# Layer one's steps in another order: turned maxima, weighted values, scores, energies

## The chip, the cores and the metric

The kernel runs on one core of one Trainium2 chip. The metric is the device time of one execution in microseconds. Three executions took 1420.77, 1421.62 and 1421.86 us; the median is 1421.62 us.

The engines have short names throughout: PE is TensorE (PEld its weight loads), DVE is VectorE, ACT is ScalarE, POOL is GpSimd, SP is SyncE, which here only issues DMAs.

## The reference

Two layers work on x with 32 batches of 128 tokens and 512 features, with a condition of 512 features per batch. Only the first layer's attention is touched by the change.

```python
def L0(hidden, w, ...):                       # layer one, 16 heads of 32 features
    h = sln(hidden, w)                        # LayerNorm, scaled and shifted by the condition
    qkv = (h @ Wqkv.T + bqkv).reshape(B, N, 16, 32, 3)
    energy = einsum('bhqd,bhkd->bhqk', q, k)
    att = softmax(energy, axis=-1) / D ** 0.5
    out = einsum('bhqk,bhkd->bhqd', att, v).reshape(B, N, D) @ Wp.T + bp
    h1 = out + hidden
    return sln(h1, w) + h1

def L1(x, cond, ...):                         # layer two, one head of 512 features, then an MLP
    x = x + attention(film(rmsnorm(x), cond)) @ proj_w + proj_b
    return x + gelu(film(rmsnorm(x), cond) @ mlp_w1 + mlp_b1) @ mlp_w2 + mlp_b2
```

## The kernel before

Batches are worked in eight groups of four (`G = 4`, `NG = 8`). Dense products are made from numbers split in two parts (a high part in a short format and the rest): `mm3` (line 152) issues three matmuls for each of four blocks of the contraction, twelve matmuls of 128x512 for one result. Layer one's attention runs over 32 steps; step `s` treats four heads of one group of four batches (`g, c = divmod(s, KC)`).

The stages of one attention step are functions, and in the same loop body stand the stages of other steps and of other batches, so that TensorE always has something to do:

- `qk0(s)` makes queries and keys of the step's four heads (24 matmuls, two ACT activations into `qk`); it runs two steps ahead. `values0(b)` makes the values of a batch, three batches ahead.
- `energies(s)` multiplies queries and keys with the query on the partitions, 16 small matmuls into four PSUM banks (`pse`), one for each head; the loop takes the four heads in turn for each batch. DVE reduces each bank to negative maxima (`nm`). It runs one step ahead.
- `totals(s, r)` lets ACT take the exponentials of one bank only for their sums: four activations with an accumulated sum each.
- `logs(s)` turns sums and maxima into one number for each row (two ACT instructions, five small ones on DVE, into `nmx`); `maxima(s)` turns that table with a TensorE transpose into the PSUM tile `psm`, and `spread_maxima(s)` copies it four times on DVE into `mT`.
- `scores0(s)` computes the same energies once more with the key on the partitions: first a matmul that subtracts the numbers of `mT`, then 16 small matmuls on top, in four banks `pst`. `exponentials(s, rs)` takes their exponentials on ACT; they are the weights, already divided.
- `heads_out(s)` multiplies weights and values (16 matmuls into one bank `pso`); `heads_high(s)` is ACT's copy of its high part, `heads_low(s)` DVE's rest of it. They are done one step later, in step `s + 1`.
- `End` is the projection of one finished batch: `stream` is a product of twelve matmuls into `psp`, `add` adds the input to it on DVE, and `first`, `sums`, `second`, `third` are the second normalization, in the step after (`past`).
- `Turned` prepares a coming batch: `stats`, `norm` on DVE with a power on POOL; `halves`, an ACT copy and a transposing DMA; a step later `merge` on DVE and four ACT activations in `rest`; a step after that `high` and `low` on DVE (`turned`).
- `Weights` prepares the second layer's weights in steps 4 to 27: `heads` copies on ACT, `tails` and `sums` work on POOL, and each head and tail is stored by a DMA on SP.

The order of instructions on PE, DVE, ACT and POOL is the order of the program (`tc.manual_schedule`); SP's DMAs are placed by a planner. The engines run in order, each waits for what its next instruction needs. A tile's buffer is taken from its pool when the program asks for it, and the first instruction that writes it waits until the last reader of the earlier tile in that buffer is done; which of the free buffers it is, the planner picks. PSUM's eight banks are three pools:

```python
ps_mm = ...tile_pool(name="ps_mm", bufs=2, ...)   # mm_tile
ps_s  = ...tile_pool(name="ps_s", bufs=2, ...)    # s_tile
ps_e  = ...tile_pool(name="ps_e", bufs=4, ...)    # e_bank
```

Before, a step asks for `pst` 0 and 1, `pso`, `psq` from `ps_mm`; for `pst` 2 and 3, `psk`, `psv` from `ps_s`; for four `pse`, `psm`, `psp` from `ps_e`.

Of the kernel before, what the change touches and what calls it, by code (L numbers as in the profile page):

```python
# [16 lines left out]
B, N, D = 32, 128, 512  # L17
P = 128
KC = D // P
# [3 lines left out]
G = 4  # L23
# [20 lines left out]
def cond_seq_kernel(ctx: ExitStack, tc, x, condT, wcond, w0, w1, wk1, wm1, wm2, cols, rows, out):  # L44
# [15 lines left out]
    def mm_tile(name):  # L60
        return ps_mm.tile([P, D], FP, tag="mm", name=name)
# [90 lines left out]
    def mm3(make, terms, done=None, by_part=False):  # L152

        if by_part:
            order = PARTS if by_part == "left" else RIGHT_LOW_LAST
            calls = [(a[pa], b[pb]) for pa, pb in order for a, b in terms]
        else:
            calls = [(a[pa], b[pb]) for a, b in terms for pa, pb in PARTS]
        n = len(calls)
        st = {}  # L160

        def call(j):
            if j == 0:
                st["ps"] = make()
            nc.tensor.matmul(st["ps"], *calls[j], start=(j == 0), stop=(j == n - 1))  # L165
            if j == n - 1 and done:
                done(st["ps"])

        return [lambda j=j: call(j) for j in range(n)]
# [9 lines left out]
    def run(*streams):  # L179

        order = sorted(
            ((j + 0.5) / len(s), i, j) for i, s in enumerate(streams) for j in range(len(s))
        )
        for _, i, j in order:
            streams[i][j]()
# [349 lines left out]
    def values0(b, by_part=False, make=None):  # L535
        g, i = divmod(b, G)
        hT = hs[0, g][0]

        def done(ps):
            if i == 0:  # L540
                vs[g] = w_tile(f"v{g}", FP)
            nc.scalar.copy(vs[g][:, i], ps)

        return mm3(
            lambda: (make or s_tile)(f"psv{b}"),
            [(sub(hT, k, ts(i, P)), sub(W0["v"], k)) for k in range(KC)],
            done, by_part,
        )

    def qk0(s, by_part=False):  # L550

        g, c = divmod(s, KC)
        hT = hs[0, g][0]
        qk[s] = d_tile(f"qk{s}", FP)
        streams = []
        for a, (nm, bias) in enumerate((("q", C_BQ0), ("k", C_BK0))):
            def done(ps, a=a, bias=bias):
                nc.scalar.activation(
                    qk[s][:, a], ps, AF.Identity, bias=col[:, bias + c : bias + c + 1], scale=1.0
                )  # L560

            streams.append(mm3(
                lambda nm=nm: (s_tile if nm == "k" and s > 1 else mm_tile)(f"ps{nm}{s}"),
                [(sub(W0[nm], k, ts(c, P)), sub(hT, k)) for k in range(KC)],
                done, by_part,
            ))
        return streams
# [89 lines left out]
    def heads_out(s):  # L657

        g, c = divmod(s, KC)
        e, v = es.pop(s), vs[g]  # L660
        if c == 0:
            os_[g] = w_pair(f"o{g}")
        pso = mm_tile(f"pso{s}")
        for i in range(G):
            for r in range(4):
                rr = slice(32 * r, 32 * r + 32)
                nc.tensor.matmul(  # L667
                    pso[rr, ts(i, P)], v[:, i, 32 * (4 * c + r) : 32 * (4 * c + r) + 32],
                    e[r][:, ts(i, P)], start=True, stop=True,
                )  # L670
        es[s] = pso
# [12 lines left out]
    class End:  # L684
# [15 lines left out]
        def stream(self):  # L700
            g, i = divmod(self.b, G)

            def done(ps):
                self.ps = ps

            return mm3(
                lambda: e_bank(f"psp{self.b}"),
                [(sub(os_[g], k, ts(i, P)), sub(W0["p"], k)) for k in range(KC)],
                done, "left" if i == 0 else False,
            )  # L710

        def add(self):
# [68 lines left out]
    def l1_vp(a, bb, c, make):  # L781

        if c == 0:
            W1["vp"] = w_pair("w1vp")
        ps = make(f"psvp{c}")
        for k in range(KC):
            nc.tensor.matmul(ps, a[:, k], bb[k], start=(k == 0), stop=(k == KC - 1))
        split_ps(W1["vp"], (slice(None), c), ps)
# [427 lines left out]
    STEPS = KC * NG  # L1216
# [14 lines left out]
    with tc.manual_schedule(engines=ordered):  # L1231
# [85 lines left out]
        new.norm()  # L1317
        run(k)
        new.halves()
        values = values0(2, make=mm_tile)  # L1320
        run(values[:4])
        maxima(0)
        spread_maxima(0)
        first[1].turn()
        run(values[4:])
        first[1].parts()
        W0["p"] = w_pair("w0p")

# [38 lines left out]
        def vp_load(c):  # L1367
            chunk[c] = l1_chunk(2, c)

        def vp(c):  # L1370
            l1_vp(chunk.pop(c), L1[3], c, s_tile if c < 3 else e_bank)

        FIRST1 = STEPS - G - 2

# [10 lines left out]
        for s in range(STEPS):  # L1385
            last = s == STEPS - 1
            end = End(s - G, True, nc.scalar) if s >= G else None
            scores0(s)
            if turned:
                turned.high(nc.vector.tensor_copy)  # L1390
                turned.low(nc.vector)
                turned = None
            if not last:
                energies(s + 1)
            exponentials(s, (0, 1))
            wn, wj = divmod(s - W_FIRST, W_STEPS)
            if 0 <= wn < KC:
                weights.heads(wj)
                weights.tails(wj)
                weights.sums(wj + 1)  # L1400
            if not last:
                totals(s + 1, 0)
            exponentials(s, (2, 3))
            if not last:
                for r in range(1, 4):
                    totals(s + 1, r)
            if s:
                heads_out(s - 1)
            if s == STEPS - 2:
                vp_load(2)  # L1410
            if past:
                past.first()
                past.sums()
            if new:
                new.stats()
            if end:
                end.bias()
                end.more()
            wn, wj = divmod(s + 1 - W_FIRST, W_STEPS)
            if 0 <= wn < KC and wj == 0:  # L1420
                weights = Weights(wn)
            if past:
                past.second()
            if ready and not last:
                ready.merge()
            if s == STEPS - 3:
                vp_load(1)
            if not last:
                logs(s + 1)
            if s:  # L1430
                heads_high(s - 1)
            q, k = qk0(s + 2, (s + 2) % KC == 0) if s + 2 < STEPS else ([], [])
            run(q)
            if staged:
                staged()
            if s < KC:
                split_w(W0["p"], raw["p"], s, nc.gpsimd)
            if s == KC + 1:
                cond_features()
            run(k)  # L1440
            if new:
                new.norm()
                new.halves()
            values = values0(s - 1 + G, make=e_bank if s < G else s_tile) if s <= B - G else []
            run(values[:9] if s < G else values)
            if s == STEPS - 3:
                vp(0)
            if s == STEPS - 2:
                vp(1)
                vp_load(3)  # L1450
                vp(2)
            if s == STEPS - 1:
                vp(3)
            if not last:
                maxima(s + 1)
                spread_maxima(s + 1)
            if s < G:
                run(values[9:])
            if s:
                heads_low(s - 1)  # L1460
            if ready and not last:
                ready.rest()
            if past:
                past.third()
            if "cq" in L1:
                L1.pop("cq")()
            staged = extras[s + 1]() if s + 1 in extras else None
            if end:
                run(end.stream())
                end.add()  # L1470
            if s == STEPS - 4:
                vp_load(0)
            coming_new = None if last else coming(s + 1)
            q2, late = divmod(s - W_FIRST, 3)
            if not late and 0 <= q2 < 4:
                nc.scalar.dma_start(out=w2d[q2], in_=wm2[:, q2])
            if not last:
                turned, ready, new = ready, new, coming_new
            past = end
            if s in CQ:  # L1480
                L1["cq"] = l1_cq(CQ.index(s))
            if s == 2:
                later["mods"] = r_tile("mods")
            if s == STEPS - 2:
                l1_load()
        heads_out(STEPS - 1)
        heads_high(STEPS - 1)
        heads_low(STEPS - 1)
        past.first()
        past.sums()  # L1490
# [191 lines left out]
```

## Time and profile before

| | |
|---|---|
| median of three executions | 1421.62 us |
| the profiled execution, time | 1421.69 us |
| its span in the profile | 1419.9 us |
| mean granted TensorE clock | 0.999 |
| busy: PE, PEld | 1402.5 us (99%), 1135.1 us (80%) |
| busy: DVE, ACT, POOL | 997.2 us (70%), 886.8 us (62%), 384.9 us (27%) |
| chain that ended last | PE 87%, DMA 4%, ACT 4%, DVE 3% |
| first score matmul of steps 0, 1, 2, 3 | 50.1, 63.2, 77.2, 92.6 us |
| of steps 4, 5, 6, 28, 31 | 107.6, 126.0, 142.8, 463.6, 510.8 us |
| `heads_out` of the last step, behind the loop | 520.4 us |

A row of the timeline or of a group names the line of the kernel, the engine, the operation, what is written and what is read (`pso<-e,v`), and the shapes. The number behind x says how many instructions a row stands for. In brackets stands the time that the engine sat idle before it, and what ended that; "issue" means that the profile shows nothing that was waited for. A row of the waits names who waited, for whom, then the total in us, the number of times and the longest. PE's matmuls overlap, and their ends are modelled, so the starts of its weight loads tell more than its busy share.

### The profile page before, as it was taken

The numbers are of one execution on the slowest core, as the hardware profiler recorded it, in microseconds if no ns is written. First come the engines' busy times: TensorE is split into PE (matmuls) and PEld (weight loads), VectorE is DVE, ScalarE is ACT, GpSimd is POOL, SyncE is SP. The second block draws the span as 40 slices with busy tenths as digits, with TensorE's granted clock in tenths as the row PEclk, the third lists the DMA queues.
The fourth block names the chain that finished last, engine by engine and source line by source line (L and its number), as shares of the span: only waits on it lengthen the run. The fifth ranks groups of instructions, "written<-read, shape, count | busy, mean of one in ns | idle before, by whom it ended". The sixth has DMA issues, their size and how long they took to land.

```text
span 1419.9 us, 25300 instructions
## 1 busy us (share of the span) xinstructions
PE 1402.5 (99%) x8968; PEld 1135.1 (80%) x8968; DVE 997.2 (70%) x1970; ACT 886.8 (62%) x2386; POOL 384.9 (27%) x361
## 2 busy tenths in 40 slices
PE   9999999999999999999999999999999999999998
PEld 5766888888888768888888888888888888888887
DVE  6666888888888887999887766665576556753342
ACT  4898899999998856677874454444453445423331
POOL 0113443535444234665541213000030003110000
PEclk9999999999999999999999999999999999999999
DMA  8359778777666557788879878576693767735350
GB/s 310 74 143 238 196 217 225 223 200 187 183 154 183 150 203 187 193 240 222 207 191 361 256 222 260 192 227 195 213 326 121 234 203 227 270 133 184 142 185 30
DMA packets 227879, 287.85 MB, mean 203 GB/s; under 512 B 107396, under 2 KB 138244, under 8 KB 226216
## 3 DMA queue, kind: packets, MB, share of 16 engines
q1 hardware_dynamic: 209888, 211.68, 51.5%
q10 hardware_dynamic: 17864, 74.55, 15.8%
q8 instruction: 70, 1.15, 0.4%
q14 instruction: 57, 0.47, 0.1%
HBM read 193.18 MB, written 73.60 MB: 188 GB/s over the span
## 4 chain that ended last, share of the span: by engine, by line
PE 87%; DMA 4%; ACT 4%; DVE 3%; issue 1%; POOL 1%; SPq 0%; ACTq 0%; POOLq 0%; DVEq 0%
PE acc L1087 24%; PE psh L165 21%; PE psp L165 6%; PE psq L165 5%; PE psk L165 5%; PE psV L165 5%; PE psv L165 5%; PE psT L165 5%; PE pso L667 2%; PE pss L848 2%; PE pse L575 2%; PE pst L644 2%; PE pso L165 1%; ACT unused L599 1%; DMA wc<-in_wcond 1%
## 5 line engine op out<-in xcount | busy, mean ns | idle before, releaser
L599 ACT ACTIVATE unused<-pse,nm 128x128 f32<-128x128 f32 x512 | 180.9, 417 | 10.3 <-DVE nm L588 7.9
L338 POOL TENSOR_TENSOR rn<-vn,neghalf 128x1 f32<-128x1 f32 x96 | 62.9, 655 | 453.3 <-DVE vn L336 346.4
L1025 ACT ACTIVATE c<-c,col 128x512 f32<-128x512 f32 x64 | 46.4, 725 | 142.3 <-DVE c L1050 89.0
L599 ACT ACTIVATION_READ_ACCUMULATOR unused<-pse,nm 128x1 f32 x512 | 131.8, 257 | 0.0
L423 ACT COPY tn<-x 128x1024 uint16<-128x1024 uint16 x90 | 94.1, 1047 | 59.2 <-DVE x L409 51.9
L432 DVE COPY tn<-tn 128x1024 uint16<-128x1024 uint16 x90 | 101.6, 1129 | 6.2 <-DMA tn<-tn 6.1
L1103 POOL TENSOR_TENSOR xe<-xe,row 128x512 f32<-128x512 f32 x32 | 45.4, 1449 | 202.8 <-DMA xe<-xs 182.9
L654 ACT ACTIVATE e<-pst 128x512 f32<-128x512 f32 x128 | 69.7, 605 | 30.1 <-PE pst L644 30.1
L588 DVE TENSOR_REDUCE nm<-pse 128x4 f32<-128x512 f32 x128 | 79.5, 684 | 11.8 <-PE pse L575 11.8
L963 POOL TENSOR_TENSOR wml<-wm,wmh 128x512 fp32r<-128x512 f32 x28 | 35.9, 1287 | 182.4 <-ACT wmh L956 154.9
L1040 DVE TENSOR_TENSOR c<-psh,ca 128x512 f32<-128x512 f32 x32 | 22.1, 692 | 86.7 <-PE psh L165 83.2
L326 DVE BATCH_NORM_STATS2 stn<-x 128x6 f32<-128x512 f32 x96 | 65.6, 683 | 2.7 <-DMA x<-in_x 2.7
L409 DVE TENSOR_SCALAR x<-x,rn 128x512 f32<-128x512 f32 x64 | 57.7, 902 | 7.4 <-POOL rn L338 6.7
L449 ACT ACTIVATE tn<-tn,mods 128x128 f32<-128x128 f32 x128 | 52.6, 483 | 11.7 <-DVE tn L432 11.7
L1053 DVE TENSOR_TENSOR ca<-psh,ca 128x512 f32<-128x512 f32 x32 | 22.1, 691 | 41.8 <-PE psh L165 41.8
L338 POOL TENSOR_TENSOR re<-ve,neghalf 128x1 f32<-128x1 f32 x32 | 31.4, 980 | 64.7 <-DVE ve L331 60.8
L1025 ACT ACTIVATE cb<-cb,col 128x512 f32<-128x512 f32 x32 | 23.2, 724 | 41.0 <-DVE cb L1054 41.0
L698 POOL TENSOR_TENSOR xe<-xe,row 128x512 f32<-128x512 f32 x32 | 44.9, 1403 | 1.7 <-DMA xe<-in_x 1.5
L1037 ACT COPY ca<-psh 128x512 f32<-128x512 f32 x32 | 18.4, 574 | 40.5 <-PE psh L165 40.0
L449 ACT ACTIVATE tn<-tn,mod 128x128 f32<-128x128 f32 x104 | 43.0, 491 | 0.0
L1107 DVE TENSOR_TENSOR xe<-acc,xe 128x512 f32<-128x512 f32 x32 | 21.1, 688 | 30.5 <-PE acc L1087 30.2
L1046 DVE TENSOR_TENSOR cb<-psh,ca 128x512 f32<-128x512 f32 x32 | 22.1, 690 | 24.8 <-PE psh L165 24.5
(1386 smaller groups left out, 4582.4 us busy)
## 6 DMA issues: line engine op xcount, KB each, us to landing
mod<-mod SPq DMA_DIRECT2D x32, 512.0 KB, 4.5
ur<-ud SPq DMA_DIRECT2D x64, 256.0 KB, 4.5
xs<-xe SPq DMA_DIRECT2D x60, 256.0 KB, 2.6
xe<-xs SPq DMA_DIRECT2D x60, 256.0 KB, 3.0
x<-xs SPq DMA_DIRECT2D x59, 256.0 KB, 3.5
scw<-scw SPq DMA_DIRECT2D x32, 256.0 KB, 3.9
hTd<-tn SPq DMA_DIRECT2D x32, 256.0 KB, 6.7
hT<-hTd SPq DMA_DIRECT2D x32, 256.0 KB, 5.1
```

The lines of the kernel that those rows point to most:

```text
L165: nc.tensor.matmul(st["ps"], *calls[j], start=(j == 0), stop=(j == n - 1))
L326: nc.vector.bn_stats(st, t)
L338: nc.gpsimd.tensor_tensor(r, v, neghalf, ALU.pow)
L409: nc.vector.tensor_scalar(X, X, r, None, ALU.mult)
L423: nc.scalar.copy(halves.rearrange("p (e d) -> p e d", e=2), X.bitcast(U16).rearrange("p (d e) -> p e d", e=2),)
L432: nc.vector.tensor_copy(self.a.bitcast(U16).rearrange("p (f e) -> p e f", e=2), self.t.bitcast(U16).rearrange("p (e f) -> p e f", e=2),)
L449: nc.scalar.activation(dst[:, c], self.a[:, ts(c, P)], AF.Identity, bias=m[:, q + B : q + B + 1], scale=m[:, q : q + 1],)
L588: nc.vector.tensor_reduce(nm[:, r], chunks(banks[r]), AX.X, ALU.max, negate=True)
L599: nc.scalar.activation(unused[s][:, ts(i, P)], banks[r][:, ts(i, P)], AF.Exp, bias=nm[:, r, i : i + 1], scale=1.0, accum_out=total[:, r, i ...
L654: nc.scalar.activation(e, es[s][r], AF.Exp)
L1025: nc.scalar.activation(t[nm], t[nm], AF.Gelu, bias=col[:, C_B1 + f : C_B1 + f + 1], scale=1.0)
L1087: nc.tensor.matmul(accs[i], u[pa][:, ts(i, P)], wb[f // 4][pb][:, f % 4, :], start=(first and j == 0), stop=(last and j == len(PARTS) - 1),)
```

## The change

The loop body of layer one's 32 steps is put in another order. A step now begins with `maxima` and `spread_maxima` of its own (before: at the end of the step before), then `heads_out`, `heads_high`, the `add` of the last step's `End`, `heads_low`; then the scores, the next energies, the four exponentials in a row and the sums in a row. Before, `heads_out` stood behind the next energies, `heads_high` behind `logs`, and `heads_low` behind the maxima at the step's end. The heads, tails and sums of `Weights` move from between the exponentials to the step's end. Three results change their PSUM pool: `pso` from `ps_mm` to `ps_e`, the keys (`psk`) from `ps_s` to `ps_mm`, the values of the first steps from `ps_e` to `ps_s`. A special order of `mm3` for the first batch of each group of `End` goes. One load (`vp_load(2)`) moves to the end of step 29, and in the part before the loop the preparation of one batch moves ahead of the values and the maxima.

```diff
     def mm3(make, terms, done=None, by_part=False):
         if by_part:
-            order = PARTS if by_part == "left" else RIGHT_LOW_LAST
-            calls = [(a[pa], b[pb]) for pa, pb in order for a, b in terms]
+            calls = [(a[pa], b[pb]) for pa, pb in RIGHT_LOW_LAST for a, b in terms]
...
-                lambda nm=nm: (s_tile if nm == "k" and s > 1 else mm_tile)(f"ps{nm}{s}"),
+                lambda nm=nm: mm_tile(f"ps{nm}{s}"),
...
-        pso = mm_tile(f"pso{s}")
+        pso = e_bank(f"pso{s}")
...
-                done, "left" if i == 0 else False,
+                done,
...
+        first[1].turn()
         values = values0(2, make=mm_tile)
-        run(values[:4])
+        run(values[:8])
         maxima(0)
         spread_maxima(0)
-        first[1].turn()
-        run(values[4:])
+        run(values[8:])
...
-            l1_vp(chunk.pop(c), L1[3], c, s_tile if c < 3 else e_bank)
+            l1_vp(chunk.pop(c), L1[3], c, mm_tile if c else s_tile)
...
         for s in range(STEPS):
             last = s == STEPS - 1
             end = End(s - G, True, nc.scalar) if s >= G else None
+            if s:
+                maxima(s)
+                spread_maxima(s)
+                heads_out(s - 1)
+                heads_high(s - 1)
+            if past:
+                past.add()
+            if s:
+                heads_low(s - 1)
             scores0(s)
...
             if not last:
                 energies(s + 1)
-            exponentials(s, (0, 1))
-            wn, wj = divmod(s - W_FIRST, W_STEPS)
-            if 0 <= wn < KC:
-                weights.heads(wj)
-                weights.tails(wj)
-                weights.sums(wj + 1)
+            exponentials(s, range(4))
             if not last:
-                totals(s + 1, 0)
-            exponentials(s, (2, 3))
-            if not last:
-                for r in range(1, 4):
+                for r in range(4):
                     totals(s + 1, r)
-            if s:
-                heads_out(s - 1)
-            if s == STEPS - 2:
-                vp_load(2)
...
                 logs(s + 1)
-            if s:
-                heads_high(s - 1)
...
-            values = values0(s - 1 + G, make=e_bank if s < G else s_tile) if s <= B - G else []
-            run(values[:9] if s < G else values)
+            if s <= B - G:
+                run(values0(s - 1 + G))
...
-            if not last:
-                maxima(s + 1)
-                spread_maxima(s + 1)
-            if s < G:
-                run(values[9:])
-            if s:
-                heads_low(s - 1)
             if ready and not last:
                 ready.rest()
...
             if end:
                 run(end.stream())
-                end.add()
             if s == STEPS - 4:
                 vp_load(0)
+            if s == STEPS - 3:
+                vp_load(2)
+            wn, wj = divmod(s - W_FIRST, W_STEPS)
+            if 0 <= wn < KC:
+                weights.heads(wj)
+                weights.tails(wj)
+                weights.sums(wj + 1)
...
         heads_out(STEPS - 1)
         heads_high(STEPS - 1)
+        past.add()
         heads_low(STEPS - 1)
```

## The prediction

> **What bounds the kernel now.** I read the page first, then the stretches of time with each engine's busy time, then the waits of one stretch, then the timeline of one step. The page says which engine to follow:
>
> ```profile
> PE 1402.5 (99%) x8968; PEld 1135.1 (80%) x8968; DVE 997.2 (70%) x1970; ACT 886.8 (62%) x2386; POOL 384.9 (27%) x361
> ```
>
> TensorE is busy 99% of the span, so only what opens a gap there, or closes one, moves the time. The change touches layer one's 32 steps, from 50 to 520 us. Step 6 to step 27 are alike: their first score matmuls stand at 142.77 and 463.60 us, 22 steps in 320.83 us, 14.58 us each.
>
> ```profile
> 142.77:463.60 320.83, 320.35 (x3279) 259.82 (x3278) 271.38 (x581) 292.85 (x1056) 143.08 (x127) 1.00 0.73 196
> ```
>
> Columns: length, then busy time of PE, PE's weight loads, DVE, ACT, POOL. Divided by 22, DVE works 12.3 and ACT 13.3 of 14.58 us. They follow TensorE closely: an order that makes them wait for each other can become the bound without any new work. The waits of this stretch:
>
> ```profile
> ACT e L654 <- PE pst L644: 22.7, 22, 2.5
> DVE xe L732 <- POOL xe L728: 14.8, 20, 1.7
> PEld psm L622 <- DVE nmx L617: 5.4, 21, 0.3
> PEld psq L165 <- ACT wmh L956: 4.2, 21, 0.2
> ```
>
> TensorE's own waits are 0.24 us a step for the maxima and 0.20 us at the next queries. ACT waits 0.7 us a step for the scores. One step in order of time, the rows that the sum needs (the first two belong to the end of the step before):
>
> ```profile
> 301.26 1.05 ACT L423 COPY tn<-x 128x1024 uint16<-128x1024 uint16 x1
> 302.68 1.66 ACT L449 ACTIVATE tn<-tn,mod 128x128 f32<-128x128 f32 x4
> 304.45 0.42 DVE L461 CAST n_20h<-tn 128x512 fp32r<-128x512 f32 x1
> 304.90 0.69 DVE L465 TENSOR_TENSOR n_20l<-tn,n_20h 128x512 fp32r<-128x512 f32 x1
> 305.99 2.48 DVE L588 TENSOR_REDUCE nm<-pse 128x4 f32<-128x512 f32 x4 [0.40 <-PE pse L575]
> 306.07 0.62 ACT L956 CAST wmh<-wm 128x512 fp32r<-128x512 f32 x1
> 306.82 1.30 POOL L963 TENSOR_TENSOR wml<-wm,wmh 128x512 fp32r<-128x512 f32 x1 [7.60 <-issue]
> 308.19 1.29 POOL L949 TENSOR_TENSOR wm<-wm 128x512 f32<-128x512 f32 x1
> 311.85 0.75 DVE L732 SCALAR_TENSOR_TENSOR xe<-te,re,xe 128x512 f32<-128x512 f32 x1 [0.69 <-POOL xe L728]
> 312.29 1.45 POOL L698 TENSOR_TENSOR xe<-xe,row 128x512 f32<-128x512 f32 x1
> 312.52 1.85 DVE L432 COPY tn<-tn 128x1024 uint16<-128x1024 uint16 x1
> 315.04 0.54 DVE L411 TENSOR_SCALAR x<-x,mvn,rn 128x512 f32<-128x512 f32 x1
> 315.62 1.05 ACT L423 COPY tn<-x 128x1024 uint16<-128x1024 uint16 x1
> ```
>
> To be seen: from the first maximum reduction (305.99) to the end of `norm` (315.04 + 0.54 = 315.58) DVE runs 9.59 us nearly without a break, and ACT's copy in `halves` follows 0.04 us later. Before, the chain ends there: what ACT does after `halves` is needed only by the next exponentials, which wait for TensorE anyway. The copy of the weighted values' high part (`heads_high`) stands early on ACT, right after `logs`.
>
> **The change, part by part.** The new order puts `heads_out`, `heads_high`, `heads_low` at the head of the step, and moves the result of `heads_out` (`pso`) from the pool of two score banks to the pool of four energy banks. That pool now serves, in order, `psm`, `pso`, four `pse`, `psp`. The four `pse` are live together, so they need all four banks: the first is free, the others come free with `spread_maxima`, `past.add` and `heads_low`, in DVE's order. So the fourth energy matmul waits for `heads_low`, whatever the planner picks. Behind it on TensorE's queue stand the rest of the energies and the step's four dense products; behind the energies, DVE's reductions.
>
> What releases `heads_low`? DVE needs ACT's `heads_high`, and that is now the last thing on ACT behind `halves`, the values' copy, the four activations of `rest` and the weight head, which the change also moves to the end of the step. So a loop closes that is open before: `heads_low`, energies, reductions, DVE's list up to `norm`, ACT's list from `halves`, `heads_high`, `heads_low`. The price of `heads_high` and `heads_low` I take from the only place where `heads_out` is already followed by them at once, the end of layer one:
>
> ```profile
> 520.43 0.81 PEld L667 LDWEIGHTS pso<-e,v 128*32 128x32 f32 x32 [0.35 <-issue]
> 521.61 0.59 ACT L676 CAST o7h<-pso 128x512 fp32r<-128x512 f32 x1 [3.21 <-PE pso L667]
> 522.22 0.69 DVE L682 TENSOR_TENSOR o7l<-pso,o7h 128x512 fp32r<-128x512 f32 x1 [0.92 <-ACT o7h L676]
> ```
>
> One turn of the loop, from one end of `heads_low` to the next:
> - `turned.high` and `turned.low` before the reductions: 304.45 to 305.59, 1.14 us. The other energies take as long beside it (their first load at 304.80, the first reduction at 305.99: 1.19, of which three matmuls are already done). With the release, 1.15.
> - reductions to the end of `norm`: 9.59.
> - to `halves`: 0.04.
> - `halves`, values' copy, `rest`: 301.26 to 302.68 + 1.66 = 304.34, 3.08.
> - the moved weight head: 0.62, of which about 0.60 passes before the next copy starts.
> - `heads_high` to the end of `heads_low`: 521.61 to 522.91, 1.30.
>
> Sum 15.76 us, against 14.58: 1.18 us a step, over 22 steps 26.0 us. Three of these steps (10, 16, 22) copy two heads; two in a row take 1.07 us in step 4, so 0.53 more: 1.6. Step 25 has no new batch and falls back to TensorE's sum (about 0.9 less), steps 26 and 27 normalize layer-two rows, whose statistics have one 0.82 us instruction instead of a 0.15 us one: together 0.7.
>
> The heads bring POOL work with them. `tails` starts 0.13 us after the head (306.69 to 306.82), takes 1.30, and `sums` another 1.29 in four steps of six. At the new place the head ends some 1.3 us before `heads_low` does, so `tails` ends about when `turned.high` (0.42) wants to start, and `sums` lies on `turned.high` and `turned.low`. Before, they lie beside reductions from PSUM. What such a meeting can cost is shown by `merge`: 1.85 us beside POOL's 1.45 us bias, and beside none
>
> ```profile
> 472.57 0.75 DVE L432 COPY tn<-tn 128x1024 uint16<-128x1024 uint16 x1
> ```
>
> Ends: 0, if they pass each other, and 1.85 - 0.75 = 1.10 a step. I take 0.5, as `tails` is nearly over and not every step has `sums`: 22 x 0.5 = 11.0; ends 0 and 24. A gain is excluded: the two rows have no POOL work beside them now.
>
> Here a rule bears on it. The Trainium skill, "SBUF — State Buffer", section "Who interferes with whom", says that VectorE and GpSimd share one port pair under an exclusive lock: whoever starts first holds it for the whole instruction, the other is shut out. It names copies and casts in a two-port mode, and instructions with two SBUF inputs while GpSimd reads SBUF; `turned.high` is the one, `turned.low` the other. The `merge` row agrees. By the rule alone `turned.high` would lose only what is left of `tails`, but `turned.low` could lose all of `sums`, an estimate of 1.3 us in four steps of six, 19 us in place of my 11.
>
> The other parts, with what hides them:
> - TensorE alone: the two waits above go (0.44). `heads_out` to the end of `heads_low` takes 522.91 - 520.43 = 2.48; TensorE gets from there to the fourth energy after 0.81 + 0.20 changeover, 1.12 of scores (303.68 to 304.80) and 0.1, that is 2.23: 0.3 us of wait if ACT is free. So TensorE's own step is 14.58 - 0.14 = 14.44; the 0.35 changeover ahead of the scores only moves ahead of `heads_out`. The spread maxima (0.69) lie beside `heads_out` (0.81 + 0.35). Hidden below 15.76.
> - Exponentials in a row: four take 2.18 (1.09 for two), then the sixteen sums: 5.74 (1.39 for four, 4.35 for twelve). `logs` is ready some 7.7 us after `heads_low`, DVE asks for it after 9.4. Hidden; 1.7 us of cover.
> - `past.add` one step later, ahead of `heads_low`: 0.69 while DVE waits for ACT. Nothing; 0.69 a step without that cover.
> - The head's two DMAs on SP (0.38 issue each) and their waits move behind the step's loads. The tail's store now stands ahead of the next step's `scw` load, which is wanted only by `third`, some ten us later: nothing. ACT's queue issues the loads of `x` and `xe` behind the head: their tiles need a free one of seven, and four or five are live: nothing, at most one load's issue, 0.5.
> - Keys to the score pool, values to the other, batch order of `psp`, `vp` banks: their banks come free with exponentials 2 us or more earlier. Nothing; the bound is the 0.20 of `psq` either way.
> - `vp_load(2)` half a step earlier and the prelude's four moved matmuls (4 x 0.227): at most 1 us either way each.
> - Outer steps. Steps 1 to 3 have no `past` and no head: the same loop is about 14.0 (the norm waits for `logs` after 8.8, ACT goes on to 12.8, then 1.3), where before they took 14.6, 15.4, 15.0: 3 us less. Steps 4, 5 and 28 to 30 carry the loop with extra work: 3 us more. Together 0, ends -3 and +6.
>
> Sum: 26.0 + 1.6 + 0.7 + 11.0 = 39.3 us. The profiled execution took 1421.69 us (span 1419.9, 1.8 outside), the median of the runs shown is 1421.62; so about 1461 us.
>
> **The rivals.**
> 1. TensorE keeps the pace. This decides if the loop falls under 14.44 us, so 1.3 us or more must leave it. For it: 0.69 us of it is DVE's wait for POOL at 311.85, and 1.10 us is `merge` held up at 312.52; shifted against POOL's bias both could go, leaving 13.97. Against it: POOL gets its work in the same order from the same DVE instructions, so the meeting should recur. Then 22 x -0.14 - 3: 1416 us, faster.
> 2. Half the loop: only one of those two goes, or no collision and a shorter ACT list. Loop 14.7 to 15.5: 1425 to 1446 us.
> 3. The collision is worse: cast and subtraction are both shut out by `tails` and `sums`, 1.1 to 1.5 us a step in place of 0.5: 1474 to 1484 us.
> 4. The change fails to create the wait, since a bank other than `heads_low`'s goes to the last `pse`. Four live tiles in four banks exclude it.
>
> The clock is no rival: from 47 to 143 us TensorE was idle 6.9 of 95.8 us and was granted 1.00. The new gaps are 1.2 to 1.7 us each; the old ones reach 1.9 us.
>
> **How the numbers follow.** My loop with its collision (1446 to 1474): 0.55; rival 3: 0.14; rival 2: 0.17; rival 1: 0.10; no change within 0.2% (about 3 us, what a measurement can tell here), where rivals 1 and 2 meet: 0.04. Predicted 1461. The range 1428 to 1484 leaves out the 0.14 of rival 1 and no change, and some 0.04 at the ends. Faster 0.10, same 0.04, slower 0.86.
>
> **What would show it.** In the changed profile: the wait of the energies' weight load for `heads_low` (a DVE subtraction out of `pso`) at some 1.2 to 1.7 us a step, 25 to 40 us in all, the largest of TensorE; steps of 15.8 to 16.3 us; ACT idle ahead of `halves` for DVE's `norm`, about 1.5 us; DVE idle ahead of `heads_low`; the waits at `psm` and `psq` gone; `turned.high` or `turned.low` longer than 0.42 and 0.69. Wrong would be: steps of 14.5 us, or a wait of the scores rather than of the energies, or ACT without idle time.

## The result, and the profile after

The changed kernel takes 1467.07 us (median of four executions, 1466.49 to 1468.39) against 1421.59 us for the kernel before (median of four): ratio 1.0322, interval 1.0304 to 1.0340. The profiled execution of it spans 1465.3 us, 45.4 us more than before.

The page of the changed kernel, its busy times and the engines' shares of the chain that ended last:

```profile
PE 1420.7 (97%) x8968; PEld 1155.0 (79%) x8968; DVE 1018.0 (69%) x1970; ACT 889.1 (61%) x2386; POOL 385.3 (26%) x361
PE 70%; DVE 8%; issue 7%; POOL 6%; ACT 5%; DMA 2%; ACTq 1%; POOLq 0%; SPq 0%; DVEq 0%
```

TensorE has the same 8968 matmuls, but its share of the chain falls from 87% to 70%: DVE, POOL, ACT and "issue" (time without a wait that the profile shows) take what it lost. By the first score matmuls of the steps, the 45.4 us lie here: up to step 6 +11.4 (154.2 against 142.8 us), steps 6 to 28 +33.6, steps 28 to 31 +0.8, all the rest -0.4. The stretch of steps 6 to 28 (length, then busy PE, weight loads, DVE, ACT, POOL, and the clock as the first number behind the counts):

```profile
154.20:508.60 354.40, 333.75 (x3282) 272.29 (x3278) 288.38 (x582) 292.12 (x1053) 144.67 (x128) 0.99 0.66 177
```

22 steps in 354.40 us are 16.11 us each, before 14.58. ACT is as busy as before (292 us, before 293); DVE is busy 17 us more (288 us, before 271) with one instruction more. TensorE, which had gaps of 0.5 us in all, has 20.7 us of them. The waits of the stretch:

```profile
ACT tn L422 <- DVE x L410: 29.4, 19, 1.6
...
DVE o5l L681 <- ACT o5h L675: 7.3, 4, 2.0
...
PEld pse L574 <- DVE o5l L681: 5.9, 4, 1.7
```

The waits for `psm` and `psq` are gone, and a new one has come: the energies' weight load waits for `heads_low` (`o5l` is one of its tiles; all of them together 23.4 us, in 16 of the 22 steps). DVE waits for `heads_high` (30.5 us over all tiles), and ACT ahead of `halves` for `norm` (29.4 us). One turn of the loop in order of time, from one `heads_low` to the next:

```profile
284.65 1.27 POOL L962 TENSOR_TENSOR wml<-wm,wmh 128x512 fp32r<-128x512 f32 x1 [5.53 <-ACT wmh L955]
...
285.08 0.69 DVE L681 TENSOR_TENSOR o3l<-pso,o3h 128x512 fp32r<-128x512 f32 x1 [1.99 <-ACT o3h L675]
...
285.69 0.50 DVE L460 CAST n_16h<-tn 128x512 fp32r<-128x512 f32 x1
285.83 0.96 PEld L574 LDWEIGHTS pse<-qk 32*128 32x128 f32 x26 [1.70 <-DVE o3l L681]
285.87 1.46 POOL L948 TENSOR_TENSOR wm<-wm 128x512 f32<-128x512 f32 x1
286.23 1.65 DVE L464 TENSOR_TENSOR n_16l<-tn,n_16h 128x512 fp32r<-128x512 f32 x1
287.80 2.47 DVE L587 TENSOR_REDUCE nm<-pse 128x4 f32<-128x512 f32 x4
...
296.86 0.55 DVE L410 TENSOR_SCALAR x<-x,mvn,rn 128x512 f32<-128x512 f32 x1
297.44 1.05 ACT L422 COPY tn<-x 128x1024 uint16<-128x1024 uint16 x1 [1.57 <-DVE x L410]
...
298.87 1.65 ACT L448 ACTIVATE tn<-tn,mod 128x128 f32<-128x128 f32 x4
...
300.42 0.61 ACT L955 CAST wmh<-wm 128x512 fp32r<-128x512 f32 x1
300.93 0.58 ACT L675 CAST o3h<-pso 128x512 fp32r<-128x512 f32 x1
...
301.54 0.69 DVE L681 TENSOR_TENSOR o3l<-pso,o3h 128x512 fp32r<-128x512 f32 x1 [0.43 <-ACT o3h L675]
```

`heads_low` ends at 285.77 and again at 302.23: 16.46 us. In between stand `turned.high` and `turned.low` (2.03 to the reductions, with `turned.low` at 1.65 us beside POOL's sums), reductions to the end of `norm` (287.80 to 297.41: 9.61), 0.03 to `halves`, ACT up to the start of `heads_high` (297.44 to 300.93: 3.49, the weight head in it), and 1.30 from there to the end of `heads_low`. The energies' load at 285.83, after 1.70 us of idling, is what TensorE pays.

### The profile page after: what moved, and what is told of

Its sections match the earlier page's. It is cut to its first block, busy times and chain, and to the rows that moved or that the text cites. A ratio compares the mean times of both kernels' runs of the same rounds, so it can differ in the third digit from the quotient of the medians.

```text
span 1465.3 us, 25322 instructions
## 1 busy us (share of the span) xinstructions
PE 1420.7 (97%) x8968; PEld 1155.0 (79%) x8968; DVE 1018.0 (69%) x1970; ACT 889.1 (61%) x2386; POOL 385.3 (26%) x361
## 3 DMA queue, kind: packets, MB, share of 16 engines
q8 instruction: 70, 1.15, 0.3%
## 4 chain that ended last, share of the span: by engine, by line
PE 70%; DVE 8%; issue 7%; POOL 6%; ACT 5%; DMA 2%; ACTq 1%; POOLq 0%; SPq 0%; DVEq 0%
PE acc L1086 24%; PE psh L164 21%; PE psV L164 6%; PE psT L164 6%; PE pss L847 2%; PE psp L164 2%; PE psq L164 2%; DVE tn L431 2%; POOL xe L727 2%; POOL wml L962 2%; PE pso L164 1%; ACT unused L598 1%; ACT tn L448 1%; POOL re L337 1%; PE psv L164 1%
## 5 line engine op out<-in xcount | busy, mean ns | idle before, releaser
L598 ACT ACTIVATION_READ_ACCUMULATOR unused<-pse,nm 128x1 f32 x512 | 126.9, 248 | 0.0
L574 PE MATMUL pse<-qk 32*128 32x128 f32 x1024 | 50.8, 297 | 26.0 <-DVE o1l L681 5.2
L653 ACT ACTIVATE e<-pst 128x512 f32<-128x512 f32 x128 | 65.9, 600 | 14.4 <-PE pst L643 14.4
L574 PEld LDWEIGHTS pse<-qk 32*128 32x128 f32 x1024 | 43.1, 201 | 31.2 <-DVE o5l L681 5.9
```

The source lines that it names most:

```text
L574: nc.tensor.matmul(banks[r][:, ts(i, P)], q[32 * r : 32 * r + 32, ts(i, P)], k[32 * r : 32 * r + 32, ts(i, P)], start=True, stop=True,)
L598: nc.scalar.activation(unused[s][:, ts(i, P)], banks[r][:, ts(i, P)], AF.Exp, bias=nm[:, r, i : i + 1], scale=1.0, accum_out=total[:, r, i ...
L653: nc.scalar.activation(e, es[s][r], AF.Exp)
```

## The experiments

All are built on one of two controls: the kernel before and the changed kernel, each with a plain DMA of the same bytes in place of the transposing one in `halves` (so the turning of the batches from the seventh on is left out). The controls take 1423.34 us (ratio to the kernel before 1.0010, 1.0001 to 1.0019) and 1466.46 us (1.0315, 1.0298 to 1.0333): they stand for the two kernels. Steps are measured between ends of `heads_low`; the changed control's are 16.43 to 16.50 us where nothing special falls into them.

**heads_high on DVE.** ACT leaves the loop.

```diff
-        nc.scalar.copy(os_[g][0][:, c], es[s])
+        nc.vector.tensor_copy(os_[g][0][:, c], es[s])
...
-                heads_high(s - 1)
             if past:
                 past.add()
             if s:
+                heads_high(s - 1)
                 heads_low(s - 1)
```

> Control of the changed kernel (plain DMA in place of the transposing one), and the high part of the weighted values copied by DVE, behind past.add, instead of by ACT. Loop theory: ACT's list behind halves leaves the loop; TensorE and DVE alone then set 15.1 us a step (3.05 from the maxima to the end of heads_low, then energies and four dense products, 12.05), up to 15.8 where the POOL collision still shifts DVE: 7 to 23 us below its control. Rival, that only the bank and the place of heads_out set the wait and ACT's tail is harmless: one more DVE instruction of 0.69 us in front of the energies, so 0 to 15 us above its control.

Measured: 1444.23 us, ratio 1.0156 (1.0133 to 1.0179), 22 us below the control. Steps of 15.15 us. The loop over ACT is real and was the longest: one copy moved to another engine, with DVE's list made longer by it, halves the loss.

**turned ahead of heads_low.** The same work on DVE, but `turned.high` and `turned.low` run while DVE waits for ACT anyway.

```diff
-            if s:
-                heads_low(s - 1)
-            scores0(s)
             if turned:
                 turned.high(nc.vector.tensor_copy)
                 turned.low(nc.vector)
                 turned = None
+            if s:
+                heads_low(s - 1)
+            scores0(s)
```

> Control of the changed kernel (plain DMA in place of the transposing one), and turned.high and turned.low in front of heads_low, in DVE's 2 us of waiting for ACT. Collision theory: POOL's tails and sums no longer hold DVE between heads_low and the reductions; in the changed kernel they cost 0.09 on each cast, 0.85 on those behind two tails and 0.95 on each subtraction beside sums, 0.87 us a step on average, 19 us over 22 steps: 15 to 21 us below its control, steps of 15.5. Rival, that the energies after the wait (1.15 us) cover the cast and subtraction anyway: within 3 us of its control.

Measured: 1460.24 us, 1.0269 (1.0249 to 1.0289), 6 us below the control: less than the 15 to 21 us of the theory and more than its rival allows. The step's price came out as the collision theory said: 15.51 to 15.57 us where the control has 16.43 to 16.50, 0.92 us less. Now DVE is first, and it is POOL that stands longer:

```profile
292.92 0.69 DVE L462 TENSOR_TENSOR n_20l<-tn,n_20h 128x512 fp32r<-128x512 f32 x1
293.01 1.73 POOL L960 TENSOR_TENSOR wml<-wm,wmh 128x512 fp32r<-128x512 f32 x1 [5.56 <-ACT wmh L953]
```

`turned.low` is back at 0.69 us, the tail takes 1.73 in place of 1.27 us, and POOL's time is not on the path. Over the 22 steps to step 28 that is 12.4 us (355.84 to 343.47), although one of them, at 16.50 us, is 1.7 us longer than in the control. Outside them 5 us are given back: step 6 comes 3.3 us later, steps 28 to 31 take 1.9 us more. What causes that isn't shown. A lower clock (0.71 in the 5 us from 100 us) stands in the first part of its trace, but the control has as much of it there: each has two stretches of 3.41 us at half clock up to step 6.

**The weights' heads, tails and sums back behind the exponentials.**

```diff
             exponentials(s, range(4))
+            wn, wj = divmod(s - W_FIRST, W_STEPS)
+            if 0 <= wn < KC:
+                weights.heads(wj)
+                weights.tails(wj)
+                weights.sums(wj + 1)
...
-            wn, wj = divmod(s - W_FIRST, W_STEPS)
-            if 0 <= wn < KC:
-                weights.heads(wj)
-                weights.tails(wj)
-                weights.sums(wj + 1)
```

> The changed kernel with the weights' heads, tails and sums put back behind the step's exponentials (left out of the computation, as in its control: the turning of batches from the seventh on, for which a plain DMA of the same bytes stands). Loop theory: ScalarE's 0.60 us for a weight head stands no longer between halves and heads_high, and the sums no longer begin beside turned.low, so that steps 6 to 28 fall from 16.1 to 14.9-15.0 us and the whole is 25 to 32 us below the control. Rival, that the loop is not closed over ScalarE and only the collision with POOL counts: 14 to 19 us below.

Measured: 1447.44 us, 1.0181 (1.0155 to 1.0206), 19 us below the control. The plain steps are 14.92 to 14.93 us, as the loop theory had them (15.53 less the head, no collision), so that theory holds for the step. The total missed the theory's 25 to 32 us and lies at the edge of the rival's range: some steps take about 15.3 us, and three take 16.8 to 17.2. Two of these three have two heads; in them ACT stood 1.5 and 1.7 us ahead of a head, once shown as waiting for the DMA of its weights, and behind it now stand the sums, `logs` and the maxima. The third follows one of them and begins at half clock (0.50 from 227.0 to 230.4 us). What makes the steps of 15.3 us is not shown. The total alone would have misled here.

**pso back in the score banks.** One line of the change undone.

```diff
-        pso = e_bank(f"pso{s}")
+        pso = mm_tile(f"pso{s}")
```

> The changed kernel with the tile of the transposed values (pso) back in the banks of the scores in place of the energies' banks (the same control and the same left out turning). Loop theory: pso then stands in the second score bank until heads_low has read it, so that now the second chunk's scores wait for heads_low by the turn of the banks; steps 6 to 28 come to 16.8-17.2 us, 15 to 25 us above the control. Rival, that the pool which the change gave to pso is the whole cause: the wait of the energies for heads_low goes and the time falls by 25 us or more.

Measured: 1500.63 us, 1.0551 (1.0528 to 1.0574), 34 us above the control. The wait only moves, from the energies to the scores:

```profile
PEld pst L637 <- DVE o5l L679: 8.6, 4, 2.5
```

No load of the energies waits for `heads_low` any more; the loads of `pst` do, 42.0 us in 22 waits from step 6 to step 28, one in each step. So the pool alone is not the cause: in the new order both pools tried for `pso` make the work that shares its bank wait. The plain steps are 16.6 us, 17.0 on the mean (16.8 to 17.2 expected). That the mean lies in the range is partly luck: six of the 22 steps hold a stretch of 3.41 us at half clock and take 17.6 to 18.2 us. The total is 9 us above what I gave it, mostly in steps 4 to 6 (18.9, 21.8 and 19.3 us), where the clock was lowered too (0.54 and 0.63 in 5 us from 100 and from 140 us).

**The heads, tails and sums at the step's end, in the kernel before.** This part of the change alone.

```diff
             exponentials(s, (0, 1))
-            wn, wj = divmod(s - W_FIRST, W_STEPS)
-            if 0 <= wn < KC:
-                weights.heads(wj)
-                weights.tails(wj)
-                weights.sums(wj + 1)
```

(The same lines, and the making of the tiles, stand at the end of the loop body.)

> The kernel before (with the same plain DMA in place of the turning one) in which one part of the change is done alone: the weights' heads, tails and sums, and the making of their tiles, stand at the end of the step instead of among the exponentials. Loop theory: without the wait of the energies for heads_low no loop is closed over ScalarE, and the head hides in its idle time; within 6 us of the kernel before. Rival, that the place of the heads and of POOL's work costs by itself: 10 to 20 us above the kernel before.

Measured: 1436.62 us, 1.0102 (1.0084 to 1.0120), 13 us above its control, as the rival had it. No loop is closed here, and still steps go from 14.54 to 15.05 us:

```profile
219.51 2.95 POOL L961 TENSOR_TENSOR wml<-wm,wmh 128x512 fp32r<-128x512 f32 x2 [5.59 <-issue]
...
219.60 1.72 DVE L463 TENSOR_TENSOR n_16l<-tn,n_16h 128x512 fp32r<-128x512 f32 x1
...
230.42 0.14 PEld L620 LDWEIGHTS psm<-ident,nmx 128*128 128x128 f32 x1 [0.78 <-DVE nmx L615]
```

POOL starts 0.09 us ahead of `turned.low` and holds it for a microsecond (1.72 in place of 0.69 us); the reductions start at once instead of after 0.39 us of waiting, the maxima come later, and TensorE stands 0.78 us ahead of `psm` in place of 0.24. So the place of the heads and of POOL's work costs by itself: 0.51 us a step, 11 us over 22 steps. The head on ACT moved too; that POOL's part is the costly one is read from these rows.

**Less weighting work in steps 0 and 1.** In the changed order DVE's `weighted` work stands ahead of `spread_maxima`.

```diff
-        weighted_more(acc, w, o, range(KC))
+        weighted_more(acc, w, o, range(1))
```

> The changed kernel in which the weighting of extras 1 and 2 (DVE's work in steps 0 and 1) is done for the first of four blocks alone: three of four DVE instructions of each are left out, beside the turning as in the control. Theory: in steps 0 and 1 the scores wait for spread_maxima behind this DVE work, so steps 0 to 1 and 1 to 2 become some 2 us shorter each, and the gap on TensorE that stands ahead of the lower clock grows shorter too: 4 to 8 us below the control. Rival, that these steps are long for another reason (the clock, or heads and norm): within 2 us of the control.

Measured: 1463.36 us, 1.0286 (1.0263 to 1.0309). The interval overlaps the control's, so the total decides nothing. In the trace the two first steps are 14.26 and 15.00 us in place of 15.98 and 15.99, so the waits are caused by that work; but at step 6 the two kernels are level again (150.47 and 150.65 us), since the first of these steps began 0.9 us later here, and in step 5 the clock was lowered here (0.50 from 135.2 to 138.6 us) and not in the control.

**High on DVE and heads back together; the weighting later as well.** The two edits shown above in one kernel, and then also

```diff
-            staged = extras[s + 1]() if s + 1 in extras else None
...
                 heads_low(s - 1)
+            staged = extras[s]() if s in extras else None
             scores0(s)
```

> The changed kernel with heads_high on VectorE and with the weights' heads, tails and sums back behind the exponentials (left out: the turning, as in its control). Loop theory: both of the links that a run alone had shortened (22 and 19 us) are gone; what is left of the loop is VectorE's list, and steps 6 to 28 fall to TensorE's own pace of 14.3 to 14.6 us, 1425 to 1435 us in all. Rival, that VectorE's list with the copy in it is as long as the loop over ScalarE was: steps of 14.9 to 15.1 us and 1440 to 1447 us.

> The same as the one with heads_high on VectorE and the weights' heads back, and the extras of a step (the weighting of steps 1 and 2 among them) stand behind heads_low of that step, as on VectorE in the kernel before, and no longer ahead of spread_maxima. Theory: TensorE's wait of about 2.4 us for spread_maxima in steps 1 and 2 goes, 4 to 6 us less than without this. Rival, that the gaps ahead of those steps come from elsewhere: within 2 us of it.

Measured: 1443.67 us, 1.0138 (1.0121 to 1.0155), and 1444.39 us, 1.0145 (1.0126 to 1.0165). Both miss what the theory gave them and lie with their rivals. The steps are 15.15 us, exactly as with `heads_high` on DVE alone. That is almost the length that the rival gave, but DVE's list alone isn't the cause, nor does ACT's `halves` play a part. One step of the first of the two:

```profile
317.41 0.69 DVE L625 TENSOR_TENSOR mT<-psm,pick 128x512 fp32r<-128x512 f32 x1 [1.03 <-PE psm L619]
...
319.33 0.69 DVE L679 TENSOR_TENSOR o4l<-pso,o4h 128x512 fp32r<-128x512 f32 x1
...
320.14 0.96 PEld L572 LDWEIGHTS pse<-qk 32*128 32x128 f32 x26 [0.40 <-PE pst L641]
320.17 1.01 PE L572 MATMUL pse<-qk 32*128 32x128 f32 x25 [0.24 <-DVE o4l L679]
```

DVE now waits 1.03 us for `psm`, that is for TensorE, and TensorE for `heads_low`: 0.24 us by the matmul's row, which names it, 0.40 by the weight load's. A third loop: spread maxima, the add, the copy and the subtraction on DVE (317.41 to 320.02, and the load at 320.14: 2.73 us; the load of the turn before stood at 304.99), then TensorE's rest of the energies and dense products up to the next `psm` (304.99 to 317.41: 12.42 us). Together 15.15. Between `psm` and the energies TensorE has only `heads_out` and the scores to do, less than DVE's four instructions take. With the copy on DVE the new order has this floor even without ACT and without POOL in the loop. The weighting put later made step 6 begin 3.2 us earlier and the total no shorter. Its trace is of the slowest of its four executions (1450.01 us, the fastest 1441.35), and shows where this one gave it back: two steps of 17.6 and 17.9 us hold 6.8 us of half clock from 224.7 us (the other kernel's trace has 3.4 us there), and in step 31 another 6.8 us follow from 535.3 us (the other has none). Whether that holds for the median is not shown.

**The maxima behind some matmuls, in the kernel before.** Could the 0.24 us wait for the maxima be had without the new order?

```diff
+            stream = end.stream() if end else []
+            run(stream[:1])
             if not last:
                 maxima(s + 1)
                 spread_maxima(s + 1)
...
-                run(end.stream())
+                run(stream[1:])
```

The second has `[:3]` and `[3:]`.

> The kernel before (with the same plain DMA in place of the turning one) in which TensorE does one of the twelve matmuls of psp, 0.39 us, ahead of the turning of the maxima; nothing else is moved. Theory: the 0.24 us in each of some 22 steps for which TensorE stood before psm is covered by that matmul, so 3 to 5 us less than its control (1423.3 us, ratio 1.001). Rival: spread_maxima on VectorE then waits longer for psm and hands the time on through heads_low to the energies' reduction, and the time stays within 1 us.

> The same with three matmuls of psp, 1.2 us, ahead of the turning of the maxima. Theory of the place: 0.24 us of wait need one matmul only; with three, spread_maxima waits some 0.8 us on VectorE in each step, of which VectorE's idle 0.2 to 0.4 us ahead of xe and of the reductions takes a part: from 4 us below to 6 us above the kernel with one matmul. Rival, that VectorE has room enough: the same time as with one matmul within 1 us.

Measured: 1423.03 us, 0.9995 (0.9986 to 1.0004), and 1423.36 us, 0.9998 (0.9988 to 1.0008): no difference from the kernel before. The wait for `psm` is gone from the trace, but the steps go from 14.54 to 14.48 us, 0.06 and not 0.24 us; over 22 steps 1.3 us. Against their control, which stood at 1.0010 but ran on another chip, the ratios are 0.0015 and 0.0012 lower, about 2 us with an uncertainty as large; a saving of 1.3 us can neither be shown nor excluded by the times. No version that ran beats the kernel before.

## Why the prediction was right, and where not

The forecast was slower, 1461 us; measured 1467.07, inside the range. The mechanism came out as forecast; that the total came so near is partly luck, since the loop was put too high and the outer steps too low. By its steps:

- **The loop.** As forecast: the energies wait for `heads_low` (1.70 us in the step shown, 1.2 to 1.7 forecast), ACT idles 1.57 us ahead of `halves`, `psm` and `psq` no longer wait, and the mean step is 16.11 us (15.8 to 16.3 forecast). Only the sum of TensorE's waits for `heads_low`, 23.4 us, is under the 25 to 40 forecast. `heads_high` on DVE showed the loop by taking ACT out. Its size without the collision is 15.51 to 15.57 us (with `turned` first), not 15.76: reductions begin 1.08 us after `heads_low` where no sums lie beside, not 1.15, and ACT from `halves` to `heads_high` takes 3.49, not 3.08 + 0.60, because I counted to the ends of instructions, and the next one starts about 0.1 us before such an end. Over steps 6 to 28 the kernel with `turned` first has 343.47 us, before 320.85: 22.6, where loop, double heads and steps 25 to 27 were to give 28.3. The last of these was wrong in sign: steps 26 and 27 (from one end of `heads_low` to the next, up to theirs) took 14.84 and 14.81 us. They have a weight head each (477.50 and 492.30 us), but ahead of 479.03 no `halves` stands in ACT's list and ahead of 493.85 no `rest`, so that ACT comes early and waits for TensorE:

```profile
479.03 0.59 ACT L675 CAST o6h<-pso 128x512 fp32r<-128x512 f32 x1 [0.91 <-PE pso L666]
...
493.85 0.59 ACT L675 CAST o6h<-pso 128x512 fp32r<-128x512 f32 x1 [0.93 <-PE pso L666]
```

The prediction saw this for the first of the two and not for the second. One reading of the profile before was off as well: ACT's wait for the scores, 22.7 us in 22 steps, is 1.0 us a step and not 0.7; nothing in the sum rests on it.
- **The collision.** Forecast 0.5 us a step in all steps, 11.0 us; measured 0.92 us in the 13 steps of 16.42 to 16.51 us and less in others, 354.92 - 343.47 = 11.4 us, or 13.1 without the one step of 16.50 us that the experiment adds (then the loop is 20.9). Sum nearly right, distribution not: `turned.low` waits out what is left of the sums (1.65 in place of 0.69 us) and `turned.high` little (0.50 in place of 0.42). That is what the Trainium skill, "SBUF — State Buffer", section "Who interferes with whom", has: whoever starts first keeps the shared pair, and the other is shut out. The order with DVE first showed the other half of it, the tail at 1.73 us. The sums stand in four steps of six, and `turned.low` is long in just these (1.64 or 1.65 us against 0.69 in the other two); each lost 0.95 us, where the prediction's estimate by the rule had 1.3.
- **The outer steps.** Forecast 0, measured +11.4 up to step 6: the step of the working that failed. I had moved the stages named in the diff and not what they were moved past: at the step's end stood also `weighted` and, ahead of the loop, one batch's turning, both DVE work that now comes ahead of `spread_maxima`. The prelude took 1.6 us more, the two steps behind it 6.0, the step from 5 to 6 4.5, the others 0.6 less. Step 0 to 1 before, where `spread_maxima` (`mT`) stands ahead of the weighting (`wwu`), and the same after the change:

```profile
62.43 0.69 DVE L628 TENSOR_TENSOR mT<-psm,pick 128x512 fp32r<-128x512 f32 x1
63.04 0.80 DVE L520 TENSOR_SCALAR wwu<-w1r,col 128x512 f32<-128x512 f32 x1
63.88 2.33 DVE L516 SCALAR_TENSOR_TENSOR wwu<-w1r,col,wwu 128x512 f32<-128x512 f32 x3
```

```profile
63.65 1.52 DVE L519 TENSOR_SCALAR wwu<-w1r,col 128x512 f32<-128x512 f32 x1
65.20 2.33 DVE L515 SCALAR_TENSOR_TENSOR wwu<-w1r,col,wwu 128x512 f32<-128x512 f32 x3
67.45 0.68 DVE L627 TENSOR_TENSOR mT<-psm,pick 128x512 fp32r<-128x512 f32 x1
68.18 0.19 PEld L639 LDWEIGHTS pst<-mT,over 32*128 32x128 f32 x4 [2.44 <-DVE mT L627]
```

- **The clock.** "The clock is no rival" was wrong for these steps. Windows of the changed kernel, the clock as the first number behind the counts of POOL:

```profile
136.00:139.00 3.00, 1.31 (x24) 1.31 (x25) 1.72 (x3) 2.55 (x5) 1.22 (x1) 0.65 0.16 48
139.00:142.00 3.00, 3.00 (x16) 2.29 (x13) 2.62 (x5) 1.89 (x11) 0.00 (x0) 0.50 0.96 386
142.00:145.00 3.00, 3.00 (x13) 2.44 (x12) 2.40 (x7) 3.00 (x19) 1.98 (x2) 0.71 1.16 281
```

After gaps of 2.68 us (ahead of 51.64) and 3.07 us (ahead of 137.69) TensorE ran at half rate. The second cost (0.35 + 0.50 + 0.29) x 3 = 3.4 us of full rate, the first 1.7 us by the same count (0.76 and 0.67 in the 3 us from 50 and from 53). Up to step 6 there are four such stretches, 8.5 us of full rate in all, against none before. The control with the plain DMA has the same order but not the stretches behind 82.5 and 134.6 us, and its step 6 comes 5.05 us earlier (150.65 against 155.70). That is close to their 1.7 + 3.4 us, but not all of it is theirs: 0.94 and 2.61 us arise in the two steps that the stretches lie in, and 1.5 us in the steps ahead of each, where a gap was already longer. So the trace shows some 3.5 us for the clock here. In the regular steps the stretches (three) cost little: the loop runs through TensorE for one microsecond only.
- **Rival 1** (TensorE keeps its pace of 14.44) could not have come true: freed of ACT and POOL in the way tried, the new order still needs 15.15. And TensorE's own step of 14.44 was put too low: in steps 26 and 27, where ACT waits for TensorE and no weight load from 466 to 495 us idles more than 0.29 us, the step is 14.8 us. I had counted `spread_maxima` as hidden beside `heads_out` and `past.add` as hidden beside ACT; with ACT out of the loop both stand in DVE's chain between `psm` and the energies.

What stays open: why `weighted` put later shortened the start but not the whole on the median, what gave back 5 us in the kernel with `turned` first, and what, beside its place in time (see the last section), makes one gap lower the clock and another not.

## What to carry to other kernels

When a tile is moved to another pool of PSUM banks, ask which later work gets its bank, and follow that wait through every engine until it closes on itself; here the loop over ACT set the step, and undoing one line only moved the wait. Cutting the longest loop shows the next: 16.45, 15.5 and 14.9 us were the loop over ACT with the collision, without it, and without the weight head too, and 15.15 us was the loop through DVE and TensorE that the copy on DVE brought. So savings measured one by one (22 and 19 us) came to 23 us together (25 by the ratios, since the two together ran on another chip). Off-path work moved on POOL can cost as much as work on the path if it meets a DVE instruction with two inputs in SBUF, and an edit to a loop body has to be checked against everything that stands between the old place and the new, in the first and last steps too.

## What the hardware showed that I had not expected

Gaps much shorter than thought were followed by a lower clock. In the changed kernel gaps on TensorE of 1.51, 1.51 and 1.57 us (ahead of 220.6, 285.8 and 367.4 us) were each followed by a mean clock of 0.72 over 6 us, which is 1.7 us of full rate lost or 3.4 us at half; others of 1.52 and 1.51 us (ahead of 318.7 and 416.8) by 1.00. In its control gaps of 2.38 and 2.67 us left the clock at 1.00. So in these traces the length of a gap does not decide alone, and the loss comes in portions of 1.7 us.

The place of a gap in time has a part in it. The seven lowered stretches of the changed kernel up to 510 us are 3.41 us long (one 6.83), and their starts (51.55, 68.62, 85.68, 136.88, 222.22, 287.07 and 368.99 us) lie whole multiples of 3.413 us apart. If the trace is cut at this distance, TensorE was busy for 0.81 to 1.90 of 3.41 us in the piece ahead of each. Two such pieces, each with the one behind it, and the two pieces that share the gap ahead of 318.7 us (the first number behind the length is PE's busy time, the clock stands as above):

```profile
218.81:222.22 3.41, 1.90 (x38) 1.53 (x34) 2.30 (x4) 2.99 (x7) 1.27 (x1) 1.00 1.05 245
222.22:225.63 3.41, 3.41 (x10) 2.63 (x9) 3.34 (x8) 3.27 (x19) 0.42 (x1) 0.50 0.94 297
283.66:287.07 3.41, 1.90 (x49) 1.59 (x46) 1.95 (x3) 3.34 (x8) 2.42 (x2) 1.00 1.12 293
287.07:290.48 3.41, 3.41 (x9) 2.67 (x10) 3.41 (x6) 1.97 (x11) 0.26 (x1) 0.50 0.95 124
314.38:317.79 3.41, 2.82 (x76) 2.20 (x74) 1.36 (x4) 3.41 (x8) 0.25 (x1) 1.00 0.82 219
317.79:321.20 3.41, 2.48 (x32) 2.15 (x33) 3.19 (x6) 2.84 (x10) 1.02 (x1) 1.00 1.03 195
```

The control's gaps of 2.38 and 2.67 us fall across such a border too (busy 2.08 and 2.35 us, 2.23 and 1.89 us). The gap ahead of 416.8 us does not (busy 1.92 us in its piece), and pieces with 1.88 and 1.62 us of work (from 184.67 and 546.48 us) were followed by no lower clock either. So where in time a gap falls fits most of these cases and not all, and no run tested it.

The Trainium skill, "TensorE: Matmul & The Clock Gate", section "HAM oscillation — how this bites in real kernels", gives as its abstract rule no idle gaps above about 3.4 us; gaps of less than half of that were enough here.
